# Seven products for all of r, z and n: the gate matmuls of a two-layer graph kernel go from 256 to 384 columns

## The chip, the cores and the metric

One core of one Trainium2 chip runs the whole kernel. The metric is the device time of one execution in microseconds (us). TensorE (PE) multiplies matrices into PSUM; VectorE (DVE), ScalarE (ACT) and GpSimd (POOL) do elementwise work; the SyncE queue (SP) issues DMAs. All data are f32.

## The reference

64 graphs of 256 nodes with 256 features go through two layers. The change touches the end of the second layer alone, a gated unit (D = 256):

```
x_in = concat([x_conv, x_nmp])                # 256 + 256 features per node
gi = x_in @ w_ih.T + b_ih                     # 768 columns: r, z, n
gh = h @ w_hh.T + b_hh                        # 768 columns: r, z, n
r = sigmoid(gi_r + gh_r);  z = sigmoid(gi_z + gh_z)
nn = tanh(gi_n + r * gh_n)
out = x + (1 - z) * nn + z * h
```

So r and z each need one sum over three kinds of input (h, x_nmp, x_conv; 768 inner rows in all), while n needs two sums kept apart: gi_n over x_nmp and x_conv, and gh_n over h alone. x_conv comes from a 17-tap convolution that the kernel does with a short Fourier transform.

## The kernel before, in words

The first 840 us prepare everything per graph and leave h, x_nmp and the layer's inputs in DRAM. Then follow four groups of 16 graphs. At a group's start, 128 transposes (`turn_outputs`) turn the group's convolution outputs into `xcT`. In groups 1 to 3 the next group's convolution follows: 32 `spectrum` steps and 24 `product` steps on PE, whose results DVE, POOL and ACT turn back in long chains of adds. Three products run before the first graph, and six in each of the next graphs (`PER = 6`, line 1601) until all 24 are done, in the fourth graph. The chains then run beside all 16 graphs.

**Order of work.** Every instruction of PE, ACT, DVE and POOL is recorded by one helper, so nearly all show line L102 in the profile, and runs on its engine in the order in which it was recorded. `after(k, go)` records `go` at the (k+1)-th `beat` from there. `beat(us)` (line 1377) then records work of the chains from five paced lines, `share * us` of estimated time for each engine; `share` is set in line 1634, and some beats take a fixed amount (`v`, `g`) off. The chains must be empty at the group's end, where `paced.drain()` (line 1614) records what is left.

**One graph** is `gates` (line 1544). With A11, A12 for the first 128 nodes and A21, A22 for the second, r and z are a 2 x 2 by 2 x 2 block product, done in seven products instead of eight. The two column halves are r and z; the inner 768 rows are split into A.1 = (h, h, first half of x_nmp) and A.2 = (x_conv, x_conv, second half of x_nmp). Each product is three matmuls of 128 x 128 by 128 x 256 (`three`, line 1463). Their inputs S1 to S4 are sums of the A parts (`gate_parts`, line 1433: `s12` on DVE, `s34` on POOL), and T1 to T4 sums of the weights (`gate_weights`, line 1408, 12 subtractions on POOL, once). The n part is not in the scheme: `gates_n` (line 1493) does six matmuls for each 128 nodes into a bank `n`. So a graph has 7 x 3 + 2 x 6 = 33 matmuls of 256 columns.

Five PSUM banks serve the gates: `ta`, `tc`, `tb`, and two of `n`; three (`ps_m`, line 1369) serve the convolution. `bank_of` (line 1478) has ACT write the biases into a bank ahead of its products, which then accumulate. ACT copies partial results out of `ta` and `tc` as `p1`, `p5`, `u2`, `u3` (256 columns each, line 1472). Three adds on DVE (`rz<-p,tb`, `rz<-u,tc`, `rz<-u,tb`) and one on POOL (`rz<-u,p`) make r and z, ACT takes their tanh, and `gates_out` (line 1508) follows with two DVE operations that read the bank `n` (`inner`), an ACT tanh (`outer`), two POOL operations (`plain`) and two on DVE (`scaled`), for each 128 nodes.

Of the kernel before, what the change touches and what calls it, by code (L numbers as in the profile page):

```python
# [185 lines left out]
def gnn_kernel(  # L186
# [18 lines left out]
    WT = N // OUT  # L205
    GROUPS = B // NG
# [27 lines left out]
    brzB = const.tile([P, 2 * D], FP, tag="brzB", name="brzB")  # L234
    bnB = const.tile([P, 2 * D], FP, tag="bnB", name="bnB")
# [311 lines left out]
    with ExitStack() as one:  # L547
# [821 lines left out]
    ps_m = ctx.enter_context(tc.tile_pool(name="ps_m", bufs=3, space=PSUM))  # L1369
    ps_gate = ctx.enter_context(tc.tile_pool(name="ps_gate", bufs=2, space=PSUM))  # L1370
# [13 lines left out]
    def outputs_turned(q):  # L1384
# [16 lines left out]
    RC, ZC = slice(0, D), slice(D, 2 * D)  # L1401
    W1 = [whT[:, 0], whT[:, 1], wiT[:, DC]]
    W2 = [wiT[:, 0], wiT[:, 1], wiT[:, DC + 1]]
    T1, T2, T3, T4 = (
        big.tile([P, 3, D], FP, tag=f"T{k}", name=f"T{k}") for k in range(1, 5)
    )

    def gate_weights():
        g = paced.on(2, "g")
        for k in range(3):  # L1410
            sub(g, T1[:, k], W1[k][:, ZC], W1[k][:, RC])
            sub(g, T2[:, k], W2[k][:, ZC], T1[:, k])
            sub(g, T3[:, k], W2[k][:, ZC], W1[k][:, ZC])
            sub(g, T4[:, k], W2[k][:, RC], T2[:, k])

# [17 lines left out]
    def gate_parts(ld, xcT):  # L1433
        n, hx = ld["n"], ld["hx"]
        base = ld["g"] * N
        xc = xcT.rearrange("p c t i -> p c (t i)")
        tok = [slice(i * P, (i + 1) * P) for i in range(NB)]
        ctok = [slice(base + i * P, base + (i + 1) * P) for i in range(NB)]
# [4 lines left out]
        ld.update(  # L1443
            A1=[[hx[:, k, t] for k in range(3)] for t in tok],
            A2=[
                [xc[:, c, t] for c in range(DC)] + [hx[:, DC + 1, tok[i]]]
                for i, t in enumerate(ctok)
            ],
            S1=S1, S2=S2, S3=S3, S4=S4,
        )  # L1450

        def s12():
            add(vec, S1[:, 0:DC], hx[:, 0:DC, tok[1]], xc[:, :, ctok[1]])
            add(vec, S1[:, DC], hx[:, DC, tok[1]], hx[:, DC + 1, tok[1]])
            sub(vec, S2, S1, hx[:, 0:3, tok[0]])

        def s34():
            sub(pool, S4[:, 0:DC], xc[:, :, ctok[0]], S2[:, 0:DC])
            sub(pool, S4[:, DC], hx[:, DC + 1, tok[0]], S2[:, DC])
            sub(pool, S3, hx[:, 0:3, tok[0]], hx[:, 0:3, tok[1]])  # L1460
        return s12, s34

    def three(dst, A, W, start):
        for k in range(3):
            pe.matmul(
                dst, A[k], W[k], start=(start and k == 0), stop=(k == 2), skip_group_check=True
            )
# [4 lines left out]
    def copied(ld, src, tag):  # L1472
        ld[tag] = t = sm2.tile([P, D], FP, tag=tag, name=f"{tag}_{ld['n']}", bufs=1)
        act.copy(t, src)
# [3 lines left out]
    def bank_of(tag):  # L1478
# [14 lines left out]
    def gates_n(ld, nb):  # L1493

        pn = ready.pop(("n", nb))
        for off, pairs in (
            (D, list(zip(ld["A1"][nb][:DC], (whT[:, c] for c in range(DC))))),
            (0, [(ld["A1"][nb][DC], wiT[:, DC])]
             + list(zip(ld["A2"][nb], (wiT[:, 0], wiT[:, 1], wiT[:, DC + 1])))),
        ):  # L1500
            for k, (a, w) in enumerate(pairs):
                pe.matmul(
                    pn[:, off : off + D], a, w[:, 2 * D :],
                    start=False, stop=(k == len(pairs) - 1), skip_group_check=True,
                )
        ld[f"pn{nb}"] = pn

    def gates_out(ld, nb):

        n, h2, x2, pn, rz = ld["n"], ld["h2"], ld["x2"], ld[f"pn{nb}"], ld["rz"][nb]  # L1510
# [3 lines left out]


        def inner():
            vec.scalar_tensor_tensor(uu, rz[:, RC], 1.0, pn[:, D:], ALU.add, ALU.mult)
            vec.scalar_tensor_tensor(uu, uu, 0.5, pn[:, 0:D], ALU.mult, ALU.add)

        def outer():  # L1520
            act.activation(nn, uu, AF.Tanh)
            ready["n", nb] = bank_of("n")
# [7 lines left out]
        def scaled():  # L1530
            vec.scalar_tensor_tensor(df, rz[:, ZC], 1.0, df, ALU.add, ALU.mult)
# [6 lines left out]

        after(2, inner)
        after(3, outer)  # L1540
        after(4, plain)
        after(5 if n == B - 1 else 6, scaled)

    def gates(ld, between, nxt):
# [4 lines left out]
        tb = ps_gate.tile([P, 2 * D], FP, tag="tb", name=f"tb_{n}", bufs=1)  # L1549
        rz = [  # L1550
            sm2.tile([P, 2 * D], FP, tag=f"rz{k}", name=f"rz_{n}_{k}", bufs=1) for k in range(NB)
        ]
        ld["rz"] = rz
        three(ta[:, RC], ld["A1"][0], [w[:, RC] for w in W1], False)
        after(1, lambda: copied(ld, ta[:, RC], "p1"))
        beat(1.3)
        three(tb[:, RC], ld["A2"][0], [w[:, RC] for w in W2], True)
        after(2, lambda: add(vec, rz[0][:, RC], ld["p1"], tb[:, RC]))
        beat(1.3)
        three(tb[:, ZC], ld["A2"][1], parts(T4), True)  # L1560
        beat(1.3)
        three(tc_[:, ZC], parts(ld["S1"]), parts(T1), False)
        after(1, lambda: copied(ld, tc_[:, ZC], "p5"))
        beat(1.3)
        between[0]()
        three(ta[:, RC], parts(ld["S2"]), parts(T2), False)
        after(1, lambda: copied(ld, ta[:, RC], "u2"))
        beat(1.3)
        three(tc_[:, ZC], parts(ld["S4"]), [w[:, ZC] for w in W2], False)

        def first_rows():
            act.activation(rz[0], rz[0], AF.Tanh, scale=0.5)
            ready["tc"] = bank_of("tc")
        after(1, lambda: add(vec, rz[0][:, ZC], ld["u2"], tc_[:, ZC]))
        after(2, first_rows)
        beat(1.3)
# [101 lines left out]
```

## Time and profile before

| | us |
|---|---|
| median of 3 runs | 2079.58 (2076.08 to 2081.04) |
| span of the profiled execution, first to last instruction | 2074.4 |
| PE busy in it | 2029.9 |
| DVE busy | 1403.6 |
| POOL busy | 1108.7 |
| ACT busy | 999.2 |
| first gate matmul of group 1, 2, 3, 4 at | 888.4, 1217.4, 1545.9, 1840.2 |

The profiled execution's own time is not listed apart from its span; its span is 5.2 us under the median of the runs, which also hold what lies before the first and after the last instruction. The profile's page has the engines' totals, the span in 40 slices, and groups of instructions. A group is named by engine, operation and `out<-in` by tile names; then come the shape, the count, the busy time, the mean of one in ns, and the idle time before with what ended it. An f32 matmul stands as two records, so `x768` is 384 matmuls. Records on one engine overlap at their ends, so the time that one instruction costs in a stream is the distance between starts, not its mean duration. The busy table by stretches gives, for chosen windows, each engine's busy time.

### The profile page before, as it was taken

The page shows a single profiled execution, that of the slowest core. Times are in us where ns is not written, and L with a number is a line of the kernel's source. Part 1 is how long each engine was busy: PE and PEld are TensorE (multiplying, and loading weights), DVE is VectorE, ACT ScalarE, POOL GpSimd, SP SyncE. Part 2 cuts the span into 40 slices and gives each one's busy share as a digit, 9 for nine tenths or more (in the row PEclk, how much of TensorE's full clock was granted, in tenths as well). Part 3 has the DMA queues.
Part 4 walks back from the last instruction along what each step waited for, and adds up shares of the span by engine and source line. Part 5 has one row for each costly group of instructions (what it writes and reads, how often), then busy time and mean ns, then how long its engine had stood idle before and what let it go on. Part 6 is the DMA issues. An engine that isn't in the chain of part 4 may idle for free. (4 is left out here: it accounts for less than half of the span.)

```text
span 2074.4 us, 31212 instructions
## 1 busy us (share of the span) xinstructions
PE 2029.9 (98%) x9977; PEld 1728.6 (83%) x9977; DVE 1403.6 (68%) x3172; ACT 999.2 (48%) x2171; POOL 1108.7 (53%) x1326
## 2 busy tenths in 40 slices
PE   7999999999999999999999999999999999999998
PEld 6877777888888787788888888888888888888887
DVE  5656666544688888237889815989924989965444
ACT  5756666665457676522344532234442234443333
POOL 4343333334775665347667527766626767644433
PEclk9999999999999999999999999999999999999999
DMA  8797987656765554656333455533446524322331
GB/s 282 261 259 245 265 257 248 208 178 224 240 206 198 178 178 138 212 178 204 122 117 117 137 176 190 168 101 118 124 152 199 155 92 129 116 87 89 95 96 61
DMA packets 292488, 352.84 MB, mean 170 GB/s; under 512 B 19523, under 2 KB 232150, under 8 KB 291670
## 3 DMA queue, kind: packets, MB, share of 16 engines
q1 hardware_dynamic: 292038, 346.40, 53.1%
q0 software_dynamic: 288, 4.46, 0.6%
q8 instruction: 80, 1.31, 0.3%
q14 instruction: 82, 0.67, 0.1%
HBM read 224.43 MB, written 126.35 MB: 169 GB/s over the span
## 5 line engine op out<-in xcount | busy, mean ns | idle before, releaser
L102 DVE TENSOR_TENSOR Xf<-y,k 128x256 f32<-128x256 f32 x184 | 69.0, 416 | 177.8 <-PE y L102 174.8
L102 DVE SCALAR_TENSOR_TENSOR Xf<-Xf 128x256 f32<-128x256 f32 (+1 forms) x248 | 185.1, 760 | 6.2 <-ACT Xf L102 5.1
L102 PE MATMUL ta<-T,S 128*128 128x256 f32 x768 | 186.6, 379 | 0.0
L102 PE MATMUL y<-wf,Xf 128*128 128x256 f32 x768 | 182.5, 380 | 1.8 <-DVE Xf L102 1.4
L102 POOL TENSOR_TENSOR rz<-u,p 128x256 f32<-128x256 f32 x64 | 47.8, 747 | 244.4 <-ACT u L102 244.4
L102 POOL TENSOR_TENSOR rs<-ve,mhalf 128x2 f32<-128x2 f32 x65 | 52.1, 801 | 220.0 <-DVE nm L102 218.7
L102 ACT ACTIVATE rz<-rz 128x512 f32<-128x512 f32 x128 | 80.3, 627 | 180.8 <-DVE rz L102 180.8
L102 PEld LDWEIGHTS y<-wf,Xf 128*128 128x128 f32 x768 | 143.9, 190 | 24.1 <-DVE Xf L102 2.6
L102 PEld LDWEIGHTS ta<-T,S 128*128 128x128 f32 x768 | 145.9, 190 | 19.8
L102 PE MATMUL n<-wiT,hx 128*128 128x256 f32 x512 | 152.3, 379 | 0.0
L102 POOL TENSOR_TENSOR xs<-Xf 128x256 f32<-128x256 f32 x92 | 69.8, 765 | 136.2 <-PE y L102 72.2
L102 DVE SCALAR_TENSOR_TENSOR h2l<-rz,h2l 128x256 f32<-128x256 f32 x128 | 102.9, 804 | 53.4 <-POOL h2l L102 53.4
L102 POOL TENSOR_TENSOR aT<-e,adjT 128x512 f32<-128x512 f32 x62 | 83.1, 1357 | 95.0 <-ACT e L102 95.0
L102 PE MATMUL ms<-wmT,h2T 128*128 128x259 f32 x512 | 127.2, 391 | 4.4 <-ACT h2T L102 4.4
L102 PE MATMUL n<-whT,hx 128*128 128x256 f32 x512 | 131.4, 379 | 0.0
L102 PE MATMUL n<-wiT,xcT 128*128 128x256 f32 x512 | 131.4, 379 | 0.0
L102 PE MATMUL nm<-aT,mso 128*128 128x256 f32 x512 | 123.3, 385 | 6.1 <-DVE pre L102 3.6
L102 PE MATMUL ag<-adjH,hs 128*128 128x256 f32 x512 | 124.3, 385 | 4.8 <-POOL adjH L102 2.7
L102 POOL TENSOR_TENSOR adjH<-adjT,eye 128x512 f32<-128x512 f32 x63 | 82.2, 1305 | 83.0 <-ACT adjT L102 81.2
L102 PE MATMUL o<-w0T,aggT 128*128 128x256 f32 x512 | 124.0, 385 | 1.4 <-ACT e L102 0.9
L102 PEld LDWEIGHTS ms<-wmT,h2T 128*128 128x128 f32 x512 | 97.8, 194 | 32.1 <-issue 12.9
L102 PE MATMUL c<-w1T,h2T 128*128 128x256 f32 x512 | 123.0, 383 | 0.0
(190 smaller groups left out, 5259.4 us busy)
## 6 DMA issues: line engine op xcount, KB each, us to landing
wf<-wfd SPq DMA_DIRECT2D x284, 256.0 KB
wfd<-fo SPq DMA_DIRECT2D x32, 576.0 KB
x2d<-x SPq DMA_DIRECT2D x64, 256.0 KB
h2d<-h SPq DMA_DIRECT2D x64, 256.0 KB
hTd<-h2T SPq DMA_DIRECT2D x64, 256.0 KB
h1d<-c1o SPq DMA_DIRECT2D x64, 256.0 KB
xnd<-xnT SPq DMA_DIRECT2D x64, 256.0 KB
h1l<-h1d SPq DMA_DIRECT2D x64, 256.0 KB
```

Of the source, the lines that this page charges most:

```text
L102: return self.tc.keep_in_program_order(getattr(self.engine, op)(*args, **kwargs))
```

## The change

The n columns join the scheme. The inner rows are now paired within each kind of input: A.1 holds the first 128 rows of h, of x_nmp and of x_conv, A.2 the second 128 of each. A block of columns is 384 wide: half of r, z and n each time, in a bank of 512 columns laid out as gi_n (`NI`, 128), r or z (`RZ`, 256) and gh_n (`NH`, 128). Matmuls with h write `HW` (the right 384), those with x_nmp and x_conv `XW` (the left 384), so both parts of n stay apart. The first half of the bank pair (`bA`) holds r, the second z.

There are again seven products, of three matmuls with 384 columns; the two that begin a fresh bank (`three_new`) split the third matmul into 256 and 128 columns. `gates_n`, the `n` banks and their bias writes are gone, and so is the POOL add. The four adds are on DVE, 512 wide, and both parts of n arrive with them in the SBUF tile `rz`, which `inner` now reads instead of PSUM. ACT's copies and bias writes are 512 wide; `p1`, `u2` and `p4` share one buffer. `ta` has two banks, `ps_m` four. The weights come in 12 DMAs instead of 2; T1 to T4 are four subtractions of 1152 columns. The beats of a graph sum to 7 x 1.95 instead of 14.3, and the shares are raised by 0.03.

The diff, with the removed bodies of `gates_n` and `gates`, which stand above, left out:

```diff
+    NI, RZ, NH = slice(0, P), slice(P, 3 * P), slice(3 * P, 4 * P)
+    XW, HW = slice(0, 3 * P), slice(P, 4 * P)
...
-            sp.dma_start(bnB[:, 0:D], b_ih[2 * D : 3 * D].partition_broadcast(P))
-            sp.dma_start(bnB[:, D:], b_hh[2 * D : 3 * D].partition_broadcast(P))
+            for b, at in ((bA, 2 * D), (bD, 2 * D + P)):
+                sp.dma_start(b[:, NI], b_ih[at : at + P].partition_broadcast(P))
+                sp.dma_start(b[:, NH], b_hh[at : at + P].partition_broadcast(P))
...
-            vec.tensor_tensor(brzB, bi, bh, ALU.add)
-
-            vec.tensor_tensor(brzB[:, D:], brzB[:, D:], brzB[:, 0:D], ALU.subtract)
+            for k, b in enumerate((bA, bD)):
+                half = slice(k * D, (k + 1) * D)
+                vec.tensor_tensor(b[:, RZ], bi[:, half], bh[:, half], ALU.add)
+
+            vec.tensor_tensor(bD, bD, bA, ALU.subtract)
...
-    ps_m = ctx.enter_context(tc.tile_pool(name="ps_m", bufs=3, space=PSUM))
-    ps_gate = ctx.enter_context(tc.tile_pool(name="ps_gate", bufs=2, space=PSUM))
+    ps_m = ctx.enter_context(tc.tile_pool(name="ps_m", bufs=4, space=PSUM))
+    ps_gate = ctx.enter_context(tc.tile_pool(name="ps_gate", bufs=1, space=PSUM))
...
-    wiT = big.tile([P, 2 * DC, 3 * D], FP, tag="wiT", name="wiT")
-    whT = big.tile([P, DC, 3 * D], FP, tag="whT", name="whT")
-    nc.sync.dma_start(whT, wh_d)
-    nc.sync.dma_start(wiT, wi_d)
...
-    W1 = [whT[:, 0], whT[:, 1], wiT[:, DC]]
-    W2 = [wiT[:, 0], wiT[:, 1], wiT[:, DC + 1]]
+    W = big.tile([P, 2, 3, 2, 3 * P], FP, tag="W", name="W")
+    for half in range(2):
+        rz, n3 = slice(half * D, (half + 1) * D), slice(2 * D + half * P, 2 * D + (half + 1) * P)
+        nc.sync.dma_start(W[:, :, 0, half, 0 : 2 * P], wh_d[:, :, rz])
+        nc.sync.dma_start(W[:, :, 0, half, 2 * P :], wh_d[:, :, n3])
+        for kind, c in ((1, DC), (2, 0)):
+            nc.sync.dma_start(W[:, :, kind, half, P:], wi_d[:, c : c + DC, rz])
+            nc.sync.dma_start(W[:, :, kind, half, 0:P], wi_d[:, c : c + DC, n3])
     T1, T2, T3, T4 = (
+        big.tile([P, 3, 3 * P], FP, tag=f"T{k}", name=f"T{k}") for k in range(1, 5)
     )
+    B11, B12, B21, B22 = (W[:, a, :, half] for a in range(2) for half in range(2))
     def gate_weights():
         g = paced.on(2, "g")
+        sub(g, T1, B12, B11)
+        sub(g, T2, B22, T1)
+        sub(g, T4, B21, T2)
+        sub(g, T3, B22, B12)
...
     def gate_parts(ld, xcT):
+        n, hx = ld["n"], ld["hx"].rearrange("p (k a) n -> p a k n", a=2)
         base = ld["g"] * N
+        xc = xcT.rearrange("p c t i -> p c (t i)")[:, :, base : base + N]
         tok = [slice(i * P, (i + 1) * P) for i in range(NB)]
         S1, S2, S3, S4 = (
             sm2.tile([P, 3, P], FP, tag=f"S{k}", name=f"S{k}_{n}", bufs=1 + (k < 3))
             for k in range(1, 5)
         )
+        for a in range(2):
+            for i, t in enumerate(tok):
+                ld[f"A{i + 1}{a + 1}"] = [hx[:, a, 0, t], hx[:, a, 1, t], xc[:, a, t]]
+        ld.update(S1=S1, S2=S2, S3=S3, S4=S4)
         def s12():
+            add(vec, S1[:, 0:2], hx[:, 0, :, tok[1]], hx[:, 1, :, tok[1]])
+            add(vec, S1[:, 2], xc[:, 0, tok[1]], xc[:, 1, tok[1]])
+            sub(vec, S2[:, 0:2], S1[:, 0:2], hx[:, 0, :, tok[0]])
+            sub(vec, S2[:, 2], S1[:, 2], xc[:, 0, tok[0]])
         def s34():
+            sub(pool, S4[:, 0:2], hx[:, 1, :, tok[0]], S2[:, 0:2])
+            sub(pool, S4[:, 2], xc[:, 1, tok[0]], S2[:, 2])
+            sub(pool, S3[:, 0:2], hx[:, 0, :, tok[0]], hx[:, 0, :, tok[1]])
+            sub(pool, S3[:, 2], xc[:, 0, tok[0]], xc[:, 0, tok[1]])
         return s12, s34
...
+    def three(bank, A, B):
+        for k, cols in enumerate((HW, XW, XW)):
+            pe.matmul(
+                bank[:, cols], A[k], B[:, k], start=False, stop=(k == 2), skip_group_check=True
+            )
+    def three_new(bank, A, B):
+        def put(cols, k, at, start, stop):
+            pe.matmul(
+                bank[:, cols], A[k], B[:, k, at], start=start, stop=stop, skip_group_check=True
+            )
+        put(XW, 1, XW, True, False)
+        put(XW, 2, XW, False, True)
+        put(RZ, 0, slice(0, 2 * P), False, True)
+        put(NH, 0, slice(2 * P, 3 * P), True, True)
...
-        t = ps_gate.tile([P, 2 * D], FP, tag=tag, name=f"{tag}_{k}", bufs=1 + (tag == "n"))
-        if tag == "n":
-            act.copy(t, bnB)
-        elif tag == "ta":
-            act.copy(t[:, RC], brzB[:, RC])
-        else:
-            act.copy(t[:, ZC], brzB[:, ZC])
+        t = ps_gate.tile([P, 2 * D], FP, tag=tag, name=f"{tag}_{k}", bufs=1 + (tag == "ta"))
+        act.copy(t, bA if tag == "ta" else bD)
...
-    def gates_n(ld, nb):
...
-        n, h2, x2, pn, rz = ld["n"], ld["h2"], ld["x2"], ld[f"pn{nb}"], ld["rz"][nb]
+        n, h2, x2, rz = ld["n"], ld["h2"], ld["x2"], ld["rz"][nb]
...
+        r, z = halves(rz[:, 0, RZ]), rz[:, 1, RZ]
+        u2 = halves(uu)
         def inner():
-            vec.scalar_tensor_tensor(uu, rz[:, RC], 1.0, pn[:, D:], ALU.add, ALU.mult)
-            vec.scalar_tensor_tensor(uu, uu, 0.5, pn[:, 0:D], ALU.mult, ALU.add)
+            vec.scalar_tensor_tensor(u2, r, 1.0, rz[:, :, NH], ALU.add, ALU.mult)
+            vec.scalar_tensor_tensor(u2, u2, 0.5, rz[:, :, NI], ALU.mult, ALU.add)
...
-            vec.scalar_tensor_tensor(df, rz[:, ZC], 1.0, df, ALU.add, ALU.mult)
+            vec.scalar_tensor_tensor(df, z, 1.0, df, ALU.add, ALU.mult)
...
+    def gates(ld, between, nxt):
+        n = ld["n"]
+        ta, tc_ = ready.pop("ta"), ready.pop("tc")
+        def new_tb(k):
+            return ps_gate.tile([P, 2 * D], FP, tag="tb", name=f"tb_{n}_{k}")
+        rz = [
+            sm2.tile([P, 2, 2 * D], FP, tag=f"rz{k}", name=f"rz_{n}_{k}", bufs=1) for k in range(NB)
+        ]
+        ld["rz"] = rz
+        part = {
+            k: sm2.tile([P, 2 * D], FP, tag=k, name=f"{k}_{n}", bufs=1) for k in ("p1", "p5")
+        }
+        part["u2"] = sm2.tile([P, 2 * D], FP, tag="p1", name=f"u2_{n}", bufs=1)
+        part["p4"] = sm2.tile([P, 2 * D], FP, tag="p1", name=f"p4_{n}", bufs=1)
+        def copied(k, src):
+            after(1, lambda: act.copy(part[k], src))
+        tanh = lambda nb: act.activation(rz[nb][:, :, RZ], rz[nb][:, :, RZ], AF.Tanh, scale=0.5)
+        def takes(k, bank):
+            ready[k] = bank_of(bank)
+        three(ta, ld["A11"], B11)
+        copied("p1", ta)
+        beat(1.95)
+        tb = new_tb(0)
+        three_new(tb, ld["A12"], B21)
+        after(1, lambda: add(vec, rz[0][:, 0], part["p1"], tb))
+        beat(1.95)
+        three(tc_, parts(ld["S1"]), T1)
+        copied("p5", tc_)
+        beat(1.95)
+        between[0]()
+        three(ta, parts(ld["S2"]), T2)
+        copied("u2", ta)
+        beat(1.95)
+        gate_rows(ld)
+        inner, outer, plain, scaled = gates_out(ld, 0)
+        three(tc_, parts(ld["S4"]), B22)
+        after(1, lambda: add(vec, rz[0][:, 1], part["u2"], tc_))
+        after(2, lambda: (tanh(0), takes("tc", "tc"), takes("ta", "ta")))
         after(2, inner)
         after(3, outer)
         after(4, plain)
+        after(5, scaled)
+        beat(1.95, v=0.2)
+        tb2 = new_tb(1)
+        three_new(tb2, ld["A22"], T4)
+        copied("p4", tb2)
+        beat(1.95, v=0.4)
         for go in between[1:]:
             go()
+        three(ta, parts(ld["S3"]), T3)
+        def second():
+            add(vec, rz[1][:, 0], part["p4"], ta)
+            add(vec, rz[1][:, 1], part["p5"], ta)
+            tanh(1)
+        inner, outer, plain, scaled = gates_out(ld, 1)
         if nxt is not None:
             after(0, nxt[0])
             after(1, nxt[1])
+        after(1, second)
+        after(2, inner)
+        after(2, outer)
+        after(3, plain)
+        after(3 if n == B - 1 else 4, scaled)
+        beat(1.95, v=0.8, g=0.7)
...
-            share[:] = (0.42, 0.55, 0.3) if todo else (0.51, 0.62, 0.3)
+            share[:] = (0.45, 0.58, 0.3) if todo else (0.54, 0.65, 0.3)
```

More of the change, by code (lines that the diff above doesn't have):

```diff
@@ L1481, in bank_of, with halves @@
         banks[tag] = k + 1
-        t = ps_gate.tile([P, 2 * D], FP, tag=tag, name=f"{tag}_{k}", bufs=1 + (tag == "n"))
-        if tag == "n":
-            act.copy(t, bnB)
-        elif tag == "ta":
-            act.copy(t[:, RC], brzB[:, RC])
-        else:
-            act.copy(t[:, ZC], brzB[:, ZC])
+        t = ps_gate.tile([P, 2 * D], FP, tag=tag, name=f"{tag}_{k}", bufs=1 + (tag == "ta"))
+        act.copy(t, bA if tag == "ta" else bD)
         return t
     ready = {}
-    def gates_n(ld, nb):
[L1495 to L1506, printed above, removed]
+    def halves(t):
+        return t.rearrange("p (h c) -> p h c", h=2)
     def gates_out(ld, nb):
-        n, h2, x2, pn, rz = ld["n"], ld["h2"], ld["x2"], ld[f"pn{nb}"], ld["rz"][nb]
+        n, h2, x2, rz = ld["n"], ld["h2"], ld["x2"], ld["rz"][nb]
         uu = sm2.tile([P, D], FP, tag="u", name=f"u_{n}_{nb}")
@@ L1541, in gates_out @@
         after(4, plain)
-        after(5 if n == B - 1 else 6, scaled)
-    def gates(ld, between, nxt):
-        n = ld["n"]
-        ta, tc_ = ready.pop("ta"), ready.pop("tc")
[L1549 to L1576, printed above, removed]
-        gate_rows(ld)
-        gates_n(ld, 0)
-        gates_out(ld, 0)
-        beat(2.6, v=0.2)
-        three(ta[:, RC], parts(ld["S3"]), parts(T3), False)
-        def second_rows():
-            copied(ld, ta[:, RC], "u3")
-            ready["ta"] = bank_of("ta")
-            add(vec, rz[1][:, RC], ld["u3"], tb[:, ZC])
-        after(1, second_rows)
-        after(2, lambda: add(pool, rz[1][:, ZC], ld["u3"], ld["p5"]))
-        after(3, lambda: act.activation(rz[1], rz[1], AF.Tanh, scale=0.5))
-        beat(1.3, v=0.4)
@@ L1597, in gates @@
             after(1, nxt[1])
-        beat(2.6, v=0.8, g=0.7)
+        after(1, second)
[4 more added lines that the diff above has]
+        beat(1.95, v=0.8, g=0.7)
     LEAD, PER = 3, 6
-    for r, tag in enumerate(("ta", "tc", "n", "n")):
-        t = ps_gate.tile([P, 2 * D], FP, tag=tag, name=f"first_{r}", bufs=1 + (tag == "n"))
+    for r, tag in enumerate(("ta", "ta", "tc")):
+        t = ps_gate.tile([P, 2 * D], FP, tag=tag, name=f"first_{r}", bufs=1 + (tag == "ta"))
         at = slice(32 * r, 32 * (r + 1))
-        pe.matmul(t, ident[at, :], brzB[at, :], start=True, stop=True)
+        pe.matmul(t, ident[at, :], bA[at, :], start=True, stop=True)
     ready["ta"], ready["tc"] = bank_of("ta"), bank_of("tc")
-    for nb in range(NB):
-        ready["n", nb] = bank_of("n")
     gate_weights()
```

40 lines of the change are left out of this document (3 added, 37 removed).

## The prediction

> **What bounds the kernel now.** First the page: engines' totals, and the row of DVE in the 40 slices (52 us each).
>
> ```profile
> PE 2029.9 (98%) x9977; PEld 1728.6 (83%) x9977; DVE 1403.6 (68%) x3172; ACT 999.2 (48%) x2171; POOL 1108.7 (53%) x1326
> ...
> DVE  5656666544688888237889815989924989965444
> ```
>
> PE is the bound on average, but DVE stands at 8 or 9 tenths in long stretches of groups 1 to 3. So I read the busy table by stretches: graph 2 of group 1 (counting from 0), graph 3, graphs 4 to 14, the gate part of graph 15, and graphs 0 to 14 of group 4. Its columns are the window, its length, then busy us and instructions of PE, PEld, DVE, ACT and POOL, then the clock granted to PE and DMA.
>
> ```profile
> 948.40:978.90 30.50, 30.05 (x140) 26.13 (x139) 25.43 (x43) 8.44 (x18) 25.27 (x27) 1.00 0.63 195
> 978.90:1000.90 22.00, 22.00 (x103) 19.37 (x102) 21.59 (x35) 6.78 (x15) 16.98 (x16) 1.00 0.56 167
> 1000.90:1159.30 158.40, 157.21 (x727) 137.77 (x726) 144.48 (x261) 63.11 (x155) 105.56 (x115) 1.00 0.36 113
> 1159.30:1173.60 14.30, 14.30 (x68) 12.52 (x68) 13.86 (x25) 6.25 (x17) 11.37 (x12) 1.00 0.34 110
> ...
> 1840.20:2053.90 213.70, 213.70 (x993) 188.13 (x992) 103.45 (x210) 74.05 (x179) 86.06 (x117) 1.00 0.29 90
> ```
>
> PE fills every stretch, at full clock (1.00). In graphs 4 to 14 DVE is busy for 144.48 of 158.4 us: 13.13 us of each graph's 14.40. Group 4, which has no convolution behind it, needs only 103.45 / 15 = 6.9 us of DVE a graph; the difference, 6.2, is paced work. Third, the timeline of PE.
>
> ```profile
> 1499.62 1.03 PE L102 MATMUL n<-whT,hx 128*128 128x256 f32 x4
> ...
> 1502.21 0.27 PE L102 MATMUL yt<-ident,Xf 128*128 128x128 f32 x1
> 1502.32 0.27 PE L102 MATMUL yt<-ident,scr 128*128 128x128 f32 x1
> ```
>
> From the first line to the transposes (yt) it issues twelve records in 2.59 us, so 0.2158 each; a 128-column record takes 0.11. No gap is left, and time goes with columns: (0.2158 - 0.109) / 128 = 0.00083 us a column.
>
> **PE's part.** Before, 66 records x 0.2158 = 14.24 us a graph, which is also 213.7 / 15. After, 19 matmuls of 384 columns (0.2158 + 128 x 0.00083 = 0.322 a record, 12.25), two of 256 (0.86) and two of 128 (0.44): 13.55. The saving is **0.69 us a graph** wherever PE stays the bound, 64 x 0.69 = 44 at most. A record of 384 columns has no row yet; strictly by columns from the 256 one it would be 0.324, which takes 0.1 a graph off the saving.
>
> **DVE's part.** Two rules of cost come from its rows and those of POOL beside it.
>
> ```profile
> 1105.60 1.85 DVE L102 SCALAR_TENSOR_TENSOR Xf<-Xf 128x256 f32<-128x256 f32 x2
> ...
> 1111.33 0.41 DVE L102 SCALAR_TENSOR_TENSOR h2l<-rz,h2l 128x256 f32<-128x256 f32 x1
> ...
> 1114.18 0.41 DVE L102 SCALAR_TENSOR_TENSOR u<-rz,n 128x256 f32<-128x256 f32 x1
> 1114.63 0.42 DVE L102 SCALAR_TENSOR_TENSOR u<-u,n 128x256 f32<-128x256 f32 x1
> 1114.97 0.41 DVE L102 TENSOR_TENSOR rz<-u,tb 128x256 f32<-128x256 f32 x1
> ```
> ```profile
> 1105.72 1.45 POOL L102 TENSOR_TENSOR hr<-hr,Xf 128x512 f32<-128x512 f32 x1
> ...
> 1114.25 0.73 POOL L102 TENSOR_TENSOR rz<-u,p 128x256 f32<-128x256 f32 x1 [3.80 <-ACT u L102]
> ```
>
> With both inputs in SBUF, an operation takes 0.41 us while POOL is idle (1111.33) and 0.93 while it works (two in 1.85 at 1105.60). With one input in PSUM it takes 0.41 either way (1114.18, beside POOL). Starts of independent ones are 0.33 apart.
>
> - *Adds.* Three of 256 columns become four of 512. The SBUF add of 512 columns on DVE, aT, took 686 ns against 418 for rz<-u,tb, so 0.27 more: 4 x 0.60 - 3 x 0.33 = **+1.4 us** a graph. All read PSUM, so there is no contention in it.
> - *s12.* Operations of 256, 128 and 384 columns become 256, 128, 256, 128: one more start, **+0.2** (0 to 0.3).
> - *inner.* Its four operations lose their PSUM input. POOL is busy for 105.56 / 158.4 = 67% of the stretch, and after losing an add (0.73) and with one more start in s34 (+0.15), about 60%: 4 x 0.6 x (0.93 - 0.41) = **+1.2** (0 to 2.1). POOL's shorter list gives back about 0.2.
>
> Here the Trainium skill speaks for the change: "VectorE: DVE Perf Modes", section "Rules for kernel authors", advises copying matmul output from PSUM to SBUF first when many operations follow. By that rule inner's term would be 0, which over 33 graphs makes the time about 40 us shorter; the rows above (0.41 with a PSUM input beside POOL, 0.93 without) say the opposite for this kernel, and I go by the rows.
>
> So in graphs 4 to 14 DVE needs 13.13 + 2.6 = **15.7 us where PE needs 13.55**. The order of instructions shows that the paced work isn't less: 10 operations a graph before and after, only its end in graph 15 moves ahead (12 operations become 8). Today DVE idles 1.27 us a graph, mostly behind POOL's h2l. When DVE is late most of this goes; I keep 0.4 (0 to 1.3). A graph takes **16.1 us in place of 14.40**: 33 graphs x 1.7 = +56.
>
> PE can't run ahead of DVE. (It shows once a group already: PE waited 1.1 us for ACT's ta at 1145, after the graph with DVE busy for 14.4 of 15.5 us.) Each engine goes in recorded order: the paced operations stand between the gate's adds; the second product in `tb` waits for the first add; the next graph's `ta` bias follows tanh on ACT, which follows the add of `tc`; and p1, u2 and p4 share a buffer, so ACT's next copy waits for a DVE add, with all later ACT work, and so the next product in `ta`, queued behind.
>
> **The other stretches.**
> - Graph 3: DVE 21.59 + 2.6 + one more paced operation (0.6) = 24.8 against 22.0: +2.8 x 3 = +8.
> - Graphs 0 to 2 (DVE at most 25.43 + 2.6 + 0.6 = 28.6 of some 29.8): -0.69 x 9 = -6.
> - Graph 15's gate part: 13.86 + 2.6 - 4 x 0.62 = 14.0 against 14.3: nothing.
> - Group 4: DVE 6.9 + 2.6 = 9.5 fits under 13.55, so 16 x -0.69 = -11. Behind the last matmul two adds and a tanh are now exposed (0.68 + 0.60 + 0.63 and small steps) that lay beside the last n matmuls: +2. Together -9.
> - A fourth bank for convolution and transposes: the waits of PE on xcT, 1 us a group's turn, shrink: -1 (-4 to 0).
>
> **Costed at nothing.** ACT: six copies or biases of 512 columns (0.58) and four tanh are 5.6 us against 5.5, of 14. Ten more weight DMAs, at about 0.42 us of SP's queue each, delay by 4.2 the loads behind them (hx, and the first h1l); that queue is empty from 849.1 to 855.1 and the first gate is at 888.4. Without this cover 4 us, once. The four T subtractions (about 2.6 us each by 0.73 for 256 and 1.26 for 512 columns) take the place of 12 (9.3 us), 20 us ahead of their use. Two more bias DMAs and one small DVE operation fall in the first stage.
>
> **Sum**, against the span of 2074.4: +56 + 8 - 6 - 9 - 1 = +48, 2122. The median stands 5.2 above that span, so **2128 us**.
>
> **The rivals.**
> 1. *PE stays the bound* (the other side: faster). It needs the growth of DVE in graphs 4 to 14 to stay under 13.55 - 13.13 = 0.42 us a graph; that is the point from which it decides. For it: PE has no stalls to speak of today, with DVE at 91%, and DVE's durations could shrink if POOL is out of step with it. Against it: the adds alone are 1.4. Price: -44 + 2 - 1, so 2037.
> 2. *Only the sure terms.* inner falls into POOL's pauses, and DVE runs without gaps: 13.13 + 1.4 + 0.2 = 14.7. Then 33 x 0.3 + 3 x 1.2 - 16 = -2: about 2077, 2062 to 2100.
> 3. *Full contention and lock-step.* Every inner operation meets POOL (+0.9) and the idle time stays (+0.9): 17.9 us, 33 x 3.5 + 14 - 16 = +114, 2194; from 2165 up.
> 4. *The change doesn't do what it says*: columns not saved. The instruction order shows 23 matmuls a graph for 33, and the rows show time by columns; no more than a few us.
>
> **The numbers.** The forecast (2100 to 2165) has 0.58, the sure terms 0.21, PE as the bound 0.14, full contention 0.07. The range, 2060 to 2170, leaves out rival 1 and most of rival 3, some 0.2. A measurement can tell about 0.3% from no change, so faster is under 2073.3, slower over 2085.8. Faster: 0.14 and a third of rival 2, 0.21. Same: 0.08, all from rival 2. Slower: 0.71.
>
> **What would show it.** Group 4 at 13.55 a graph shows PE's step. In graphs 4 to 14: DVE over 97% busy and PE waiting at ta, tb or tc for ACT or DVE; u<-rz and u<-u,rz at a mean near 0.7 us; adds at 0.68. If the u rows stay at 0.42, or the stretch is below 150 us, the DVE step was wrong. If PE waits in group 4 as well, the shared buffer or the longer ACT chain costs more than I allowed.

## The result and the profile after

The changed kernel takes **2113.89 us** (median of 4 runs, 2112.98 to 2117.03); the kernel before took 2077.85 on the same chip (2076.08 to 2081.04, 4 runs). The ratio is 1.0178, 95% interval 1.0164 to 1.0193. The profiled execution has a span of 2112.2 us, 37.8 more than before. The forecast was 2128, in a range of 2060 to 2170.

First the page: the totals of the engines, and DVE in the 40 slices.

```profile
PE 2012.5 (95%) x8695; PEld 1469.6 (70%) x8695; DVE 1489.2 (71%) x3301; ACT 1004.3 (48%) x2041; POOL 1077.7 (51%) x1318
...
DVE  5666666444687887249999726999934999985555
```

PE does 17.4 us less than before (2029.9 then) and DVE 85.6 us more (1403.6). The new thing is in the slices: DVE's row now holds three runs of 9s, one in each of groups 1 to 3. The busy table shows what they mean. The stretches are graph 3 of group 1, graphs 4 to 14 of group 1, and graphs 0 to 14 of group 4; the columns are as before.

```profile
980.00:1001.30 21.30, 21.30 (x83) 15.27 (x82) 19.80 (x30) 6.60 (x13) 14.82 (x16) 1.00 0.49 161
...
1001.30:1176.50 175.20, 159.13 (x508) 94.61 (x507) 162.34 (x293) 63.67 (x133) 102.06 (x117) 0.96 0.31 99
...
1886.70:2090.20 203.50, 203.50 (x692) 126.45 (x691) 117.20 (x239) 76.85 (x149) 77.20 (x117) 1.00 0.30 95
```

Group 4 does what the change says: 203.5 us for 15 graphs, 13.57 each, in place of 213.7, with PE filled. Graph 3 is filled too (21.30 of 21.30), and shorter than before (22.0). In graphs 4 to 14 the stretch grew from 158.4 to 175.2 us, and PE, which had 157.21 of the 158.4, is busy for only 159.13 of it. The lines of PE name where (busy time, mean ns, then the waiting time and what ended it, all over the span):

```profile
L102 PE MATMUL ta<-T,S 128*128 128x384 f32 x768 | 275.8, 496 | 21.6 <-ACT p L102 21.6
...
L102 PE MATMUL ta<-W,hx 128*128 128x384 f32 x256 | 100.3, 517 | 26.9 <-ACT ta L102 26.9
```

Both waits are for a copy on ACT: the bias of the next graph's `ta`, and the copy `p` (p1) that must be taken out of `ta` before the fourth product (S2) goes on in that bank. ACT is far from full (63.67 of 175.2 us), so the question is whom ACT waited for. One such wait, from the timeline of graph 7 of group 1:

```profile
1055.68 2.10 PE L102 MATMUL tc<-W,S 128*128 128x384 f32 x6
...
1060.02 1.48 DVE L102 TENSOR_TENSOR Xf<-Xf,hr 128x256 f32<-128x256 f32 x1
...
1061.42 0.74 DVE L102 SCALAR_TENSOR_TENSOR Xf<-Xf 128x256 f32<-128x256 f32 x2
...
1062.54 0.68 DVE L102 TENSOR_TENSOR rz<-u,tc 128x512 f32<-128x512 f32 x1
...
1063.26 0.63 ACT L102 ACTIVATE rz<-rz 128x512 f32<-128x512 f32 x1 [1.00 <-DVE rz L102]
...
1064.31 0.58 ACT L102 COPY ta<-bA 128x512 f32<-128x512 f32 x1
...
1064.94 2.40 PE L102 MATMUL ta<-W,hx 128*128 128x384 f32 x4 [3.04 <-ACT ta L102]
```

PE ends the fifth product (S4, into `tc`) at 1057.78. The add that reads it, `rz<-u,tc`, starts at 1062.54, since DVE goes in recorded order and works without a gap through the operations that stand ahead of it, the last of them the paced Xf. That is 4.8 us; ACT's tanh and the biases of `tc` and `ta` behind the add take 1.7 more, and PE goes on after a wait of 3.04. (All nine waits of PE in these graphs that last 2.9 to 3.8 us have a stretch at half clock with them; the last section has its figures.)

By stretch, summed over the groups, the 37.8 us come from:

| stretch | before | after | difference | forecast |
|---|---|---|---|---|
| up to the first gate matmul | 888.4 | 891.4 | +3.0 | 0 (4 without cover) |
| graphs 0 to 2 of groups 1 to 3 | 270.9 | 266.4 | -4.4 | -6 |
| graph 3 | 66.0 | 64.0 | -2.0 | +8 |
| graphs 4 to 14 (33 graphs) | 475.2 | 524.2 | +49.0 | +56 |
| graph 15 with the turns | 139.6 | 140.8 | +1.1 | -1 |
| group 4 | 234.2 | 225.4 | -8.8 | -9 |

### The profile page after: what moved, and what is told of

Read it like the earlier page. It is cut to its first block, busy times and chain, and to the rows that moved or that the text cites. A ratio compares the mean times of both kernels' runs of the same rounds, so it can differ in the third digit from the quotient of the medians.

```text
span 2112.2 us, 28763 instructions
## 1 busy us (share of the span) xinstructions
PE 2012.5 (95%) x8695; PEld 1469.6 (70%) x8695; DVE 1489.2 (71%) x3301; ACT 1004.3 (48%) x2041; POOL 1077.7 (51%) x1318
## 5 line engine op out<-in xcount | busy, mean ns | idle before, releaser
L102 PE MATMUL ta<-T,S 128*128 128x384 f32 x768 | 275.8, 496 | 21.6 <-ACT p L102 21.6
L102 POOL TENSOR_TENSOR S<-hx,S 128x256 f32<-128x256 f32 x64 | 53.8, 840 | 304.1 <-PE ta L102 214.7
L102 DVE SCALAR_TENSOR_TENSOR Xf<-Xf 128x256 f32<-128x256 f32 (+1 forms) x248 | 162.5, 674 | 11.8 <-ACT Xf L102 10.7
L102 POOL TENSOR_TENSOR h2l<-h2l,nn 128x256 f32<-128x256 f32 x127 | 111.5, 878 | 65.4 <-ACT nn L102 65.4
L102 PE MATMUL tc<-W,S 128*128 128x384 f32 x384 | 134.8, 488 | 0.0
L102 PE MATMUL tc<-T,S 128*128 128x384 f32 x384 | 134.5, 486 | 0.0
L102 PE MATMUL ta<-W,hx 128*128 128x384 f32 x256 | 100.3, 517 | 26.9 <-ACT ta L102 26.9
```

Of the source, the lines that this page charges most:

```text
L102: return self.tc.keep_in_program_order(getattr(self.engine, op)(*args, **kwargs))
```

## The experiments

**Theory A**: DVE has no time left in graphs 3 to 15 of groups 1 to 3. Its work there sets the length, and in whatever order that work stands, PE waits. **Rival B**: DVE has time enough on average; the order on ACT's queue makes PE wait, because a copy that PE needs stands behind a tanh that needs a late add. **Rival C**: the raised shares bring the paced work into these graphs too early.

For all runs, one table of groups 1 to 3, graphs 3 to 15, from the traces: the length, DVE's busy time in it, the rest (DVE's idle time), and the time at which PE's first gate matmul starts. "Ratio" is to the kernel before on the same chip, with its 95% interval.

| kernel | median | ratio | graphs 3 to 15 | DVE busy | DVE idle | first gate |
|---|---|---|---|---|---|---|
| before | 2077.9 | | 680.9 | 569.5 | 111.4 | 888.4 |
| after | 2113.9 | 1.0178 (1.0164 to 1.0193) | 729.0 | 621.6 | 107.4 | 891.4 |
| early_ta | 2118.5 | 1.0193 (1.0176 to 1.0210) | 729.3 | 621.1 | 108.1 | 893.4 |
| p1_first | 2117.7 | 1.0175 (1.0149 to 1.0201) | 732.8 | 633.8 | 98.9 | 893.0 |
| both_orders | 2108.2 | 1.0139 (1.0124 to 1.0154) | 722.0 | 632.4 | 89.6 | 892.4 |
| old_shares | 2120.3 | 1.0196 (1.0181 to 1.0212) | 732.5 | 626.1 | 106.4 | 891.0 |
| less_inner | 2083.5 | 1.0022 (1.0012 to 1.0031) | 697.7 | 592.4 | 105.3 | 892.6 |
| act_instead | 2098.0 | 1.0094 (1.0080 to 1.0108) | 710.8 | 587.7 | 123.0 | 890.6 |
| no_plain | 2066.8 | 0.9940 (0.9923 to 0.9956) | 682.9 | 568.3 | 114.6 | 893.0 |
| pool_add | 2181.9 | 1.0503 (1.0486 to 1.0520) | 792.8 | 593.6 | 199.2 | 895.7 |
| weight_layout | 2110.4 | 1.0155 (1.0140 to 1.0171) | 728.5 | 622.0 | 106.5 | 888.1 |
| hybrid | 2076.3 | 0.9994 (0.9984 to 1.0003) | 689.7 | 568.3 | 121.4 | 894.7 |
| hybrid2 | 2076.3 | 0.9994 (0.9986 to 1.0003) | 693.7 | 568.5 | 125.2 | 887.6 |
| last_group | 2067.6 | 0.9951 (0.9937 to 0.9964) | 680.0 | 555.5 | 124.5 | 890.7 |

### The order of the copies: early_ta, p1_first, both_orders

early_ta lets ACT write the bias of the next `ta` one beat earlier, ahead of the tanh:

```diff
-        after(2, lambda: (tanh(0), takes("tc", "tc"), takes("ta", "ta")))
+        after(1, lambda: takes("ta", "ta"))
+        after(2, lambda: (tanh(0), takes("tc", "tc")))
```

> One line moved in the changed kernel: ACT writes the next graph's biases into the other ta bank one beat earlier, ahead of the tanh of the first rows, so it no longer waits for DVE's add of tc. DVE's work and order are the same. Theory A (DVE is out of time: its work in graphs 4 to 14 needs more than PE's 13.56 us): PE only waits at another bank, the time stays within 8 us of 2114. Rival B (an order of ACT's queue that puts a copy which PE needs behind work that waits for a late DVE; DVE itself is idle 7% of these graphs): the 27 us that PE waits for ta's biases go, and with them most of the 14 us that the halved clock costs after such waits: 2080 to 2095.

p1_first moves the end of the second rows one beat back, so that the next graph's copy of p1 stands ahead of nn on ACT:

```diff
-        after(2, outer)
-        after(3, plain)
-        after(3 if n == B - 1 else 4, scaled)
+        after(3, outer)
+        after(4, plain)
+        after(4 if n == B - 1 else 5, scaled)
```

> One beat later for the second rows' last steps in the changed kernel: ACT's copy p1 of the next graph is recorded ahead of the tanh nn of the second rows, which waits for inner on DVE. DVE's work is the same, scaled of the second rows comes one beat later. Theory A: within 8 us of 2114. Rival B: the 21.6 us that PE waits for p before the product with S2 go, and 5 us of halved clock after the three long ones: 2090 to 2104.

both_orders has both edits.

> early_ta and p1_first together. Theory A: PE's waits turn up at tb and tc, over 2100. Rival B: PE is held only by DVE's own sum of work, 14.76 us a graph in graphs 4 to 14 against 15.89 now, so at most 37 us less: 2077 to 2088, no halved clock in these graphs.

Each edit does take away the wait that it aims at, and the wait comes back elsewhere. In the kernel after PE waited 26.9 us at `ta<-W,hx` and 21.6 at `ta<-T,S`; in early_ta the first is gone and the second is 44.5; in p1_first the second is gone and the first is 39.9. Neither is faster; both_orders wins 6 us of the 36 (8 by the ratios), and its waits come back at `tb` and `tc`, as theory A expected. It cuts graphs 4 to 14 by 22.3 us (524.2 to 501.9), but gives back 5.4 in graph 3 and 9.9 in graph 15. The table says why: DVE's idle time falls from 107.4 to 89.6, and its busy time rises from 621.6 to 632.4 with the same instructions. The commonest paced operation on DVE, first in the kernel after and then in both_orders (count, busy time, mean ns, idle time before):

```profile
L102 DVE SCALAR_TENSOR_TENSOR Xf<-Xf 128x256 f32<-128x256 f32 x220 | 141.0, 662 | 11.8 <-ACT Xf L102 10.7
```

```profile
L102 DVE SCALAR_TENSOR_TENSOR Xf<-Xf 128x256 f32<-128x256 f32 x220 | 161.9, 755 | 6.3 <-ACT Xf L102 5.6
```

What the better order closes, 17.8 us of idle time, comes back as 10.8 us of slower operations. So B holds for single waits and for some 6 us; in the orders tried it doesn't explain the other 30.

### The shares: old_shares

```diff
-            share[:] = (0.45, 0.58, 0.3) if todo else (0.54, 0.65, 0.3)
+            share[:] = (0.42, 0.55, 0.3) if todo else (0.51, 0.62, 0.3)
```

> The changed kernel with the shares of paced work as before (0.51 and 0.42 for DVE instead of 0.54 and 0.45). Theory A (DVE's sum of work in graphs 3 to 15 sets the time): the paced work only moves from graph to graph and to the group's end, 2108 to 2122. Rival C (the raised shares are what makes PE wait): the waits of graphs 4 to 14 shrink and the time falls below 2100.

Graphs 4 to 14 fall to 506.5 us, but graph 15, where what is left of the paced work must end, grows from 140.8 to 162.0. Nothing is won (ratio 1.0196), and rival C falls.

### Less work on DVE: less_inner, act_instead, no_plain

less_inner leaves the second operation of `inner` out:

```diff
-            vec.scalar_tensor_tensor(u2, u2, 0.5, rz[:, :, NI], ALU.mult, ALU.add)
```

> The changed kernel without the second operation of inner: gi_n is left out of n, so two DVE operations of 0.67 us in the mean are gone from each graph. The order of the rest is unchanged. Theory A: 33 graphs x 1.3 us of DVE time, 42 us, and the halved clock goes too: 2060 to 2072. Rival B: the waits for p shrink by the 0.6 to 1.3 us that stood ahead of nn, those for ta by little since the add of tc stays behind the paced work: 2085 to 2105.

act_instead gives one of the four adds to ACT as a plain copy:

```diff
-            add(vec, rz[1][:, 1], part["p5"], ta)
+            act.copy(rz[1][:, 1], ta)
```

> The changed kernel with one of its four additions a graph given to ScalarE as a plain copy out of the bank of ta: the second block of the second rows is copied instead of added to p, so the product p5 is left out of that block of z and of what is formed from it. VectorE does about 0.6 us a graph less in graphs 3 to 14 and ScalarE about 0.58 us more, in the same place of the chain. Theory A (VectorE is out of time): graphs 4 to 14 lose about 0.6 us each over 33 graphs, 20 us, and the time is 2090 to 2100. Rival B (the order of ScalarE's queue sets the time): ScalarE has more in the chain, so nothing is won, 2108 to 2125. Rival C (the raised shares): also about 2108 to 2118.

act_instead came within theory A's range. less_inner, at 2083.5, came in neither: 11.5 us above A's and 1.5 under B's, and PE's wait at `ta<-W,hx` stayed (25.6 us of 26.9), as B said. The table still speaks for A: without the inner operation DVE is busy for 29.2 us less in graphs 3 to 15, they are 31.3 shorter, and the time falls by 30. With the copy on ACT the time falls by 16, to 2098, though the copy sits in the very chain that rival B blames; here DVE's busy time falls by 33.9 and half of it (15.6) turns into idle time, so the order holds back part of the gain.

no_plain leaves POOL's two `plain` operations for each half graph out, and touches no instruction of DVE except in the last half graph:

```diff
-            e = vec if n == B - 1 and nb == NB - 1 else pool
-            e.tensor_tensor(df, df, nn, ALU.subtract)
-            e.tensor_tensor(ot, ot, nn, ALU.add)
+            return
```

> The changed kernel without POOL's two operations plain (h minus nn, x plus nn) for each half graph: the outputs lack nn. DVE, ACT and PE keep every instruction. POOL loses about 3.5 us of 9.2 a graph. If POOL beside DVE is what makes DVE's two-SBUF operations slow: those of inner, scaled and the paced work shorten by about 1 us a graph together, 33 us or more off: 2065 to 2090. If the contention is no part of it, DVE's durations stay and the time is within 6 us of 2114, since DVE waits for POOL's h2l for next to nothing in the changed kernel.

DVE's busy time in graphs 3 to 15 falls from 621.6 to 568.3 with its own instructions unchanged, and the time by 47 us, below that of the kernel before. (Stretches at half clock shrink as well when DVE has less to do: behind the first gate matmul 45.1 us in the kernel after, 24.4 in act_instead, 19.6 in less_inner and 14.9 in no_plain. How much of each gain came by way of the clock isn't told apart.) The two `u` operations in it, from DVE's groups by form:

```profile
L102 DVE SCALAR_TENSOR_TENSOR u<-u,rz 128x256 f32<-128x256 f32 x128 | 77.1, 603 | 4.4
...
L102 DVE SCALAR_TENSOR_TENSOR u<-rz 128x256 f32<-128x256 f32 x128 | 61.3, 479 | 39.5 <-ACT rz L102 38.1
```

To be read beside those of the kernel after (`rz<-p,ta` reads PSUM, and is 680 ns here as in no_plain, 682):

```profile
L102 DVE SCALAR_TENSOR_TENSOR u<-u,rz 128x256 f32<-128x256 f32 x128 | 85.3, 666 | 4.4
L102 DVE TENSOR_TENSOR rz<-p,ta 128x512 f32<-128x512 f32 x128 | 81.9, 680 | 13.8 <-PE ta L102 13.5
L102 DVE SCALAR_TENSOR_TENSOR u<-rz 128x256 f32<-128x256 f32 x128 | 76.4, 597 | 39.1 <-ACT rz L102 37.7
```

and of the kernel before, where the two `u` operations read `n` in PSUM:

```profile
L102 DVE SCALAR_TENSOR_TENSOR u<-u,n 128x256 f32<-128x256 f32 x128 | 53.8, 421 | 4.4
L102 DVE SCALAR_TENSOR_TENSOR u<-rz,n 128x256 f32<-128x256 f32 x128 | 53.1, 415 | 64.2 <-PE n L102 61.0 <-ACT rz L102 3.1
```

The operations with both inputs in SBUF get shorter when POOL does less (h2l too, from 679 to 489); the ones with a PSUM input do not move. Sorted by whether POOL was at work within 0.2 us of their start, the `u` operations of the kernel after take 424 and 425 ns beside an idle POOL, 745 and 940 beside a busy one; in the kernel before they took 413 to 421 either way. This is what the Trainium skill states in "SBUF — State Buffer", section "Who interferes with whom": an instruction of VectorE with two SBUF inputs contends with one of GpSimd that reads SBUF, and one with at most one SBUF input, outside the 2-port perf modes, does not. The rows agree.

### An add on POOL: pool_add

The fourth add goes to POOL, where an add stood before the change. ACT first copies `ta` into SBUF for it; the second rows come one beat later, and S1 and S2 have one buffer each to make room:

```diff
-            add(vec, rz[1][:, 1], part["p5"], ta)
-            tanh(1)
+            u3 = sm2.tile([P, 2 * D], FP, tag="u3", name=f"u3_{n}", bufs=1)
+            act.copy(u3, ta)
+            add(pool, rz[1][:, 1], part["p5"], u3)
...
+        after(2, lambda: tanh(1))
+        after(3, inner)
+        after(3, outer)
+        after(4, plain)
+        after(4 if n == B - 1 else 5, scaled)
```

> One DVE add of 512 columns a graph (p5 + ta) goes back to POOL, as its half was before: ACT copies ta into SBUF, POOL adds, and the tanh of the second rows with all that follows comes one beat later. DVE loses 0.6 us a graph, POOL gains about 1.4, ACT 0.6. Theory A: 33 x 0.6 = 20 us less DVE work, of which POOL's longer list gives back some through slower DVE operations with two SBUF inputs: 2094 to 2106. If POOL's work costs DVE as much as it saves, 2110 to 2120.

This missed by far: 2181.9. DVE has 28 us less to do in graphs 3 to 15, but stands for 92 us more. One chain, from the timeline:

```profile
1062.45 1.27 POOL L102 TENSOR_TENSOR rz<-p,u 128x512 f32<-128x512 f32 x1
...
1063.75 0.63 ACT L102 ACTIVATE rz<-rz 128x512 f32<-128x512 f32 x1 [2.57 <-POOL rz L102]
...
1065.20 0.43 DVE L102 SCALAR_TENSOR_TENSOR Xf<-Xf 128x256 f32<-128x256 f32 x1 [3.71 <-ACT Xf L102]
...
1069.18 0.42 ACT L102 ACTIVATE nn<-u 128x256 f32<-128x256 f32 x1 [3.71 <-DVE u L102]
...
1069.81 0.56 ACT L102 COPY p<-tc 128x512 f32<-128x512 f32 x1
...
1070.52 1.62 PE L102 MATMUL tc<-W,S 128*128 128x384 f32 x2 [3.41 <-ACT p L102]
```

ACT's tanh waits 2.57 us for POOL's add; the paced Xf behind it on ACT comes late; DVE, in recorded order, waits 3.71 us for that; so u and nn are late, the copy of `p` stands behind nn, and PE waits 3.41 us. Here rival B is right: a chain through POOL, ACT and DVE in strict order can cost more than DVE's whole excess. Whether the single buffers of S1 and S2 add to it isn't told apart. Theory A needs that limit: less work on DVE helps as long as the order lets it.

### The start: weight_layout

Stage one writes the scratch copy of the weights in the order of use (`w_d`), and one DMA replaces the twelve:

```diff
-    for half in range(2):
...
-            nc.sync.dma_start(W[:, :, kind, half, 0:P], wi_d[:, c : c + DC, n3])
+    nc.sync.dma_start(W.rearrange("p a k h c -> p (a k h c)"), w_d)
```

> The changed kernel, with the scratch copy of the weights written in stage one in the order in which the graphs use it, so that it comes back in one transfer with long rows instead of 12 with short ones; nothing else is changed. If the 3.0 us later first gate of the changed kernel is due to the 12 transfers, the first gate comes at 888 to 889 us and the time falls by about 3 us, to about 2111; if it is due to the fourth bank or the clock, the first gate stays at 891 to 892 and the time at 2114.

The first gate comes at 888.1, and the median falls by 3.4 us, as that theory said, though the intervals of the two ratios overlap (1.0140 to 1.0171, and 1.0164 to 1.0193). The waits of PE from 835 to 892 us, in the kernel after and here (us in all, times, longest):

```profile
PE df L102 <- DMA h1l<-h1d: 3.5, 2, 3.1
```

```profile
PE df L102 <- DMA h1l<-h1d: 1.5, 3, 1.0
```

In all ten kernels with the twelve DMAs of the change this wait is 3.1 to 4.9 us; in the three with one DMA (this one, hybrid2, last_group) it is 0.4 to 1.5. The time of the first gate also holds what varied before this stage; from PE's `first` matmuls, at 842.7 to 846.3, to the first gate it is 46.7 to 50.2 us in the ten and 43.8 to 44.9 in the three (45.2 before the change). That is why last_group's first gate comes at 890.7 all the same. The ten also have 3.41 or 6.83 us at half clock beginning between 859 and 864, and the three have none there.

### The change only where DVE has time: hybrid, hybrid2, last_group

hybrid works as before the change in graphs 3 to 15 of groups 1 to 3 and in the last graph, with the two products of n in banks of `ps_m`; its n lacks part of its bias. hybrid2 is the same with two `n` banks of their own and the weights as in weight_layout. last_group keeps the change only for graphs 0 to 14 of group 4, and in the other graphs ACT writes only the 256 bias columns that they use, as before (hybrid2 wrote 512). The choice, as hybrid2 has it (hybrid writes the same in one line):

```diff
+    def is_plain(n):
+        return n >= B - 1 or (n < B - NG and n % NG >= 3)
...
-            gates(ld, between, nxt)
+            (gates_rz if plainly else gates)(ld, between, nxt)
```

Here `gates_rz` has the old steps, with the old products cut out of `W`. From hybrid2 to last_group:

```diff
-        return n >= B - 1 or (n < B - NG and n % NG >= 3)
+        return n >= B - 1 or n < B - NG
...
-        act.copy(t, bias)
+        act.copy(t[:, cols], bias[:, cols])
```

> Graphs 0 to 2 of groups 1 to 3 and all of group 4 but its last graph go as in the changed kernel. Graphs 3 to 15 of groups 1 to 3 and the last graph of all go as before: 256 columns, n apart in PSUM, three DVE adds and one on POOL, the shares of before, with the new pairing and weight layout. Theory A: these graphs take 14.4 us again, and the 24 others keep 0.69 each, less 3 us at the start: 2079 - 16 + 3 - 1, 2062 to 2069. If the layout, the pairing or the weight loads were what costs, it stays above 2085.

> Graphs 3 to 15 of groups 1 to 3 and the last graph of all work as before the change, with n's own two products in a bank of its own; graphs 0 to 2 of each group and all of group 4 but the last work by the change; the weights' scratch is written in the order of use. Where VectorE has time for the additions the change is worth the 0.69 us of TensorE that the products save: 24 graphs by 0.69 is 16.5 us. Theory A: graphs 4 to 14 run at 14.4 us as before, the last graph as before, and the time is 2060 to 2067. If the change costs something where VectorE has room as well, or the second set of n's sums delays the start by more than 6 us, the time is 2070 to 2080, no better than before.

> Only the first 15 graphs of the last group work by the change (beside their steps no graph network's work is paced); all graphs of groups 1 to 3 and the last graph of all work as before the change, with the half bank of bias copies of before (hybrid2 copied whole banks there, 0.22 us more for each of two copies in ScalarE's chain); the weights' scratch is in the order of use. Theory A: graphs 48 to 62 take 203.5 us instead of 213.7, groups 1 to 3 the times of before (graphs 4 to 14 475 to 478 us in all, where hybrid2 had 484.7), so 10 us less, 2065 to 2069, ratio 0.993 to 0.996. If the time is 2074 or more, the change costs something even where its additions do not matter, or the waits of hybrid2 came from something other than the longer copies, and graphs 4 to 14 stay above 482.

hybrid and hybrid2 give no difference that can be told from the kernel before, and so miss theory A's ranges; hybrid2 lies in that of a change that costs something where DVE has room too. The gain of group 4 is there (203.5 in place of 213.7), but graphs 4 to 14 take 482.8 and 484.7 us in place of 475.2. In hybrid2 three graphs of each group (4, 8 and above all 10, with 16.25 us for 14.24) hold most of the excess; one of them ends like this:

```profile
1100.08 0.63 ACT L102 ACTIVATE rz<-rz 128x512 f32<-128x512 f32 x1 [5.95 <-DVE rz L102]
...
1101.53 0.59 ACT L102 COPY ta<-bA 128x512 f32<-128x512 f32 x1
...
1102.17 1.13 PE L102 MATMUL ta<-W,hx 128*128 128x256 f32 x4 [1.84 <-ACT ta L102]
```

The bias of `ta` stands third behind a late tanh, and PE waits 1.84 us. last_group has none of the excess: its graphs 4 to 14 take 475.3 us, and group 4 keeps the gain:

```profile
1003.02:1161.47 158.45, 157.00 (x727) 137.77 (x726) 140.92 (x274) 63.33 (x155) 109.70 (x127) 1.00 0.35 112
1843.23:2046.71 203.48, 203.48 (x693) 126.42 (x692) 117.78 (x239) 76.40 (x149) 77.56 (x117) 1.00 0.30 95
```

It takes **2067.56 us, ratio 0.9951 (0.9937 to 0.9964)**, and beats both kernels. Whether the longer copies or the changed graphs 0 to 2 ahead of them caused hybrid2's waits isn't told apart, since last_group differs in both.

## Why the prediction was right, and where its sizes were off

The side and the mechanism were right: PE's saving shows only where DVE has room, and in graphs 4 to 14 DVE takes over as the bound. It isn't as full there as the sign named, though: busy for 93% (14.78 of 15.89 us), not over 97%. By its steps:

- **PE's part**, 0.69 us a graph: 0.68 in group 4 (10.2 / 15). Right, and the 384-column record came at the length worked out.
- **DVE's part** in graphs 4 to 14, busy us a graph. Adds: forecast +1.4, measured +1.41. s12: +0.2, measured +0.05. inner: +1.2, measured +1.03 (1.52 to 2.55). The mis-sized term is the relief: POOL's shorter list "gives back about 0.2", and the relief was about 0.86: h2l, x2l and the paced operations, most with two SBUF inputs, went from 9.28 to 8.42. POOL's list is little shorter (316.6 to 305.2 us), but it is spread over a stretch that grew, so its share fell from 67 to 58% (the prediction had about 60%, but put only 0.2 on what the rest gains by it). So DVE does 14.78 a graph, not 15.7.
- **Idle time** of DVE, forecast 0.4 (0 to 1.3): measured 1.11, against 1.27 before. The step "when DVE is late most of this goes" failed. The graphs don't share one length: 5, 6 and 12 run at 13.56 to 13.59, PE's own pace, and 4, 7, 8, 10, 11 and 13 at 15.4 to 19.3, with waits of PE of up to 3.8 us. DVE's longest wait of before, in graphs 4 to 14 of group 1 (us in all, times, longest),

```profile
DVE h2l L102 <- POOL h2l L102: 7.7, 7, 1.8
```

is gone as forecast, but others took its place, for ACT's part of the paced chains, for a tanh, and for PE's products:

```profile
DVE Xf L102 <- ACT Xf L102: 3.1, 3, 1.3
DVE u L102 <- ACT rz L102: 2.3, 6, 0.7
DVE rz L102 <- PE tc L102: 2.2, 2, 1.8
```

both_orders shows that part of it is order (89.6 us in place of 107.4).
- The two errors have opposite signs, so that **16.1 us a graph**, measured 15.89, is right by more luck than working: 33 x 0.21 = 7 of the 10 us that the sum was too high. The other 4 us by which 2128 is over 2113.89 are the 5.2 added for what a run holds beyond the span: here the median stands 1.7 above it. The 5.2 set the median beside the span of a faster execution.
- **Graph 3**, +8: measured -2.0. PE runs through it at its own pace, and DVE's arrears are paid in graph 4, which grew from 14.24 to about 19. Part of the +49 is this term, in another place.
- **Graphs 0 to 2** and **group 4** came as forecast (-4.4 and -8.8 for -6 and -9), the tail with +1.4 for -0.69 + 2.
- **Costed at nothing**: the weight DMAs. The cover that the text named failed, 3.0 us were lost at the start, and weight_layout gives them back. The -1 for the fourth bank didn't show: at the turns of groups 2 to 4 PE waited only 0.34 us for `xcT` before, not 1, and waits 2.1 now.

Of the rivals, "PE stays the bound" needed less than 0.42 us of growth on DVE; it grew by 1.64. "Only the sure terms" had DVE at 14.7, which is nearly what it came to, but only because inner's growth, which it put at nothing, and the relief nearly cancel; with no idle time left in it, its 2077 was too low. The advice of the Trainium skill that the prediction weighed ("VectorE: DVE Perf Modes", section "Rules for kernel authors") didn't hold here: the `u` operations went from 415 and 421 ns to 597 and 666.

## What to carry to other kernels

Before moving work from the bounding engine, read in the stage itself how much room the next one has: here 0.42 us a graph, against 1.64 of new work. An operation moved from a PSUM input to two SBUF inputs must be priced beside what GpSimd does at the time, and so must all others of its kind on that engine, since each of them gets shorter or longer with GpSimd's share. Where a kernel's stages differ, a change may be worth making only in the stage that has room: here the 15 graphs of group 4 that take it gave 10.2 us, and that is the gain of the one kernel of these that does the whole work and is faster than before.

## What the runs showed of the hardware

- In graphs 4 to 14 of the kernel after, each of PE's nine waits of 2.9 to 3.8 us has a stretch at half clock with it, which begins between 0.7 us before the wait's end and 1.3 us after; the waits of up to 1.6 us have none. With the wait that ended at 1064.94 (above) the granted clock is 0.50 for 3.41 us, from 1065.52, and PE's first records take 2.40 us for four, as the timeline's last line has it, where they took 1.45 in the first graph. The kernel after has 45.1 us at half clock behind the first gate matmul, before had 5.6. The Trainium skill, "TensorE: Matmul & The Clock Gate", section "What's actually happening", has the clock halved after an idle window of about 3.4 us, the windows running freely. The stretches here are one or two times 3.41 us long, which agrees; but the 3.41 us before 1065.52 held 2.8 us of waiting and 0.6 of work, so here the window was not wholly idle, and in pool_add a wait of 3.41 us, ended at 1542.71, has no such stretch. It costs less than it seems: both_orders has 18.9 us of it and is only 6 us faster.
- Closing idle time on DVE made its operations longer (Xf from 662 to 755 ns), as more of them met POOL (160 of the 220 within 0.2 us of their start, in place of 135). Its busy time isn't a property of its instructions alone.
- Twelve loads with short rows took SP's queue until 853.7, with the loads of `hx` and `h1l` behind them. The first `h1l` load behind them is issued at 855.39, only 0.28 us later than before (855.11), but PE's wait for `h1l` lasts 3.1 us and ends at 860.39, with the DMA engines busy throughout (share 1.00 from 856.0 to 860.4). So the late issue alone doesn't make the 3 us; which of the transfers under way held it up isn't told apart.
